# Projecting queries and keys by batch, 256 columns at a time, in the opening of two attentions

## The chip, the cores and the metric

The kernel runs on one core of a Trainium2 chip, all in float32 but for a few small bfloat16 terms. The metric is the device time of one execution in microseconds (us), taken as the median of several runs. Beside it stands one execution taken by the hardware profiler, from which every duration below comes. Engines are called as the profile calls them: PE (TensorE, matrix products), PEld (its weight loads, which overlap the products), DVE (VectorE), ACT (ScalarE), POOL (GpSimd) and SP (SyncE, which only issues transfers here).

## The reference

Two decoder layers on x of 8 batches x 256 tokens x 512 features, each step followed by a residual and a layer norm. What matters here is the first step of each layer:

```
def reference(x, ...):
    x = _layernorm(x + _L0_attn_ref(x, Wq, Wk, Wv, Wo, ...))     # first attention (differential)
    x = _layernorm(x + _L0_xattn_ref(...))                       # long convolution
    x = _layernorm(x + _L0_ffn_ref(x, ...))                      # mixture of experts, top 2 of 8
    x = _layernorm(x + _L1_attn_ref(x, w_qkv, w_o))              # self attention
    x = _layernorm(x + _L1_xattn_ref(...))
    x = _layernorm(x + _L1_ffn_ref(...))

# both attentions, per batch:
    q, k, v = projections of x          # 512 query features; keys and values 128 (first) or 512 (self)
    scores = q @ k.T * HD ** -0.5, masked above the diagonal
    out = softmax(scores) @ v           # first: attn1 - lambda * attn2, then an rms norm
    return out @ Wo.T
```

## The kernel before, in words

**Tiles.** The 2048 tokens are 16 tiles of 128 (`x[t]`), two tiles to a batch, and four tiles, which are two batches, to a group (`TPG` = 4, `GT` = 512 columns, `NG` = 4 groups, `S` = 256). To project a group, PE turns each of its tiles (`turned_group`, L194), ACT copies the turned tile into `xT` (L195; one buffer), and then a block of 128 features for the whole group is four products of 128x512 accumulated in PSUM (`feature_block`, L1404, through `product_steps`, L175) and evacuated by ACT (L1411). On PE each float32 product is two instructions in the profile. `token_block` makes the values of one tile.

**The attention loop.** `causal_attention` runs over units, a unit being some heads of one batch: 16 units to a group in the first attention (`upb` = 8 a batch), 8 in the self attention (`upb` = 4). A unit goes through `maxima` (L1151: scores `ps_q` on PE; L1160: ACT copies them into `rows`; L1162: POOL masks; L1171: DVE takes the maxima `neg`), some units later `weights` (L1214, L1223: scores again with the maxima subtracted, L1231: exponential on ACT, L1232 and L1242: mask and sum on POOL) and `products` (L1257, L1267: values and row sums on PE; L1275: DVE's reciprocal). The scores have one PSUM buffer. `rows` has two buffers in the first attention and one in the self attention, so there ACT's copy of a unit waits until DVE has reduced the unit before. After the maxima of a whole batch, DVE splits them (`split`) and PE turns them (`turn`, L1193).

**Order by hand.** Within the loop PE, DVE, ACT and POOL keep the order in which the program writes the instructions (`manual_schedule`); SP is free. Between the pieces of a unit, `fill(budget)` takes projection steps from `queue`, a list of pieces with the unit (slot) at which each is due; `MM` = 0.86 and `TR` = 0.45 are the costs that the planner counts for a product of 512 columns and a tile's transposes. `pressure` raises the budget when due times are near, `need(slot)` forces what is due, and `at(slots, place, f)` hangs a call on a later unit. `begin(g + 1)` puts the next group's pieces into the queue half way through a group. A queue that is empty leaves a unit with nothing between its parts.

**Opening of the first attention** (`diff_attention`). SP issues, in order: four x tiles (`load_x(range(TPG))`), Wk, Wq, Wv, Wo, small tables, the other twelve tiles. DVE and POOL reorder the columns of Wq once it is there (L269, L271). PE turns four tiles, projects the keys of the group (`ps_k`) and the first query block (`ps_f`), and begins the first unit's scores.

**Opening of the self attention.** Its x is not in SBUF: `combine` brings a tile back (`load`: x from `xd` through SP, L1075, and two gathers of 128 rows of the experts' results from `ys`, issued by POOL, L1077), adds the two results (`add`: DVE L1086, with the norm's moments and POOL's L139 and L140) and normalizes (`norm`: DVE L154). The first four tiles are brought before the loop begins, their steps interleaved; those of the next group hang on units of the loop:

```
        for steps in zip(*[arrive(t) for t in range(TPG)]):
            for f in steps:
                f()
...
                    first = max(0, 2 * KB * g - 1 + ti)
                    at(first - here, "end", load)
                    at(first - here + 1, "mid", lambda add=add: add(lambda f: at(0, "end", f)))
                    at(first - here + 2, "mid", norm)
```

Then come 4 query and 4 key blocks of 512 columns, due pairwise at units 0 to 3 of the group, and values due at 5 and 7 (9 in the last group).

Of the kernel before, what the change touches and what calls it, by code (L numbers as in the profile page):

```python
# [5 lines left out]


# [2 lines left out]

# [6 lines left out]
F32 = mybir.dt.float32  # L17
# [6 lines left out]
P = 128  # L24
B, S, D = 8, 256, 512
NT = B * S // P
TPG = 4
NG = NT // TPG
GT = TPG * P
KB = D // P  # L30
# [19 lines left out]
def decoder_kernel(ctx: ExitStack, tc: tile.TileContext, a: dict, out: bass.AP):  # L50
# [17 lines left out]
        for t in tiles:  # L68
            nc.sync.dma_start(out=x[t], in_=xin[:, t, :])

    load_x(range(TPG))

    ident = const.tile([P, P], F32, tag="ident", name="ident")
    make_identity(nc, ident)
# [97 lines left out]

    MM, TR = 0.86, 0.45

    def product_steps(tile, lhsT, rhs, done):  # L175

        ps = []

        def step(k):
            if k == 0:  # L180
                ps.append(tile())
            nc.tensor.matmul(  # L182
                ps[0], lhsT=lhsT(k), rhs=rhs(k), start=(k == 0), stop=(k == KB - 1)
            )
            if k == KB - 1:
                done(ps[0])

        return [(MM, lambda k=k: step(k)) for k in range(KB)]

    def turned(pools, dst, src, tag="mm"):  # L190

# [43 lines left out]
    def diff_attention():  # L235
# [6 lines left out]
        w = wpool.tile([P, 7168], F32, tag="w", name="w_l0")  # L242
        wk = load_w(w, 2048, a["L0_attn_Wk"], P)
        wq_in = load_w(w, 0, a["L0_attn_Wq"], D)
        wv = load_w(w, 2560, a["L0_attn_Wv"], P)
        wo = w[:, 3072:5120].rearrange("p (k c) -> p k c", k=KB)
        for t in range(4):
# [51 lines left out]
        def prepare(work, pools, g, at, here):  # L299
            qT = work.tile([P, KB, GT], F32, tag="qT", name="qT")  # L300
            kz = work.tile([P, 2, GT], F32, tag="kz", name="kz")
            v = work.tile([P, TPG, P], F32, tag="v", name="v", bufs=3)
            xT, need = turned_group(work, pools, g)

            def values(ti, ps=[]):
                if ti == 0:
# [7 lines left out]
                    nc.scalar.copy(v, ps.pop())  # L314

            values_steps = [(MM, lambda ti=ti: values(ti)) for ti in range(TPG)]
            if g:

                need.append((0, values_steps))

            def keys(ps):
                for i in range(2):
                    nc.scalar.mul(kz[:, i, :], ps, half[:, i : i + 1])

            need.append(
                (
                    0,
                    product_steps(
                        lambda: pools.tile([P, GT], F32, tag="mm", name="ps_k"),
                        lambda k: wk[:, k, :],  # L330
                        lambda k: xT[0][:, k, :],
                        keys,
                    ),
                )
            )
# [761 lines left out]
    def causal_attention(name, prepare, finish, upb=KB, gather=None):  # L1097
# [18 lines left out]
        with ExitStack() as st:  # L1116
# [176 lines left out]

            def at(slots, place, f):

                if place == "fill":
                    after.append((now[0] + slots, f))
                    after.sort(key=lambda piece: piece[0])
                else:
                    events.setdefault((now[0] + slots, place), []).append(f)  # L1300
# [100 lines left out]
                fill(9.0)  # L1401
                happen("end")

    def feature_block(pools, r, xT, w, at, c, scale=1.0):  # L1404

        cs = slice(at + c * P, at + (c + 1) * P)
        return product_steps(
            lambda: pools.tile([P, GT], F32, tag="mm", name="ps_f"),
            lambda k: w[:, k, cs],
            lambda k: xT[0][:, k, :],  # L1410
            lambda ps: nc.scalar.mul(r[:, c, :], ps, scale),  # L1411
        )

    def token_block(pools, xT, w, at, ti, done):
# [21 lines left out]

    def self_attention(wqkv, wo, arrive):

        for steps in zip(*[arrive(t) for t in range(TPG)]):
            for f in steps:  # L1440
                f()

        def prepare(work, pools, g, at, here):
            qT = work.tile([P, KB, GT], F32, tag="qT", name="qT")
            kT = work.tile([P, KB, GT], F32, tag="kT", name="kT")
            v = work.tile([P, TPG, D], F32, tag="v", name="v_s")
            xT, need = turned_group(work, pools, g)
            for c in range(KB):
                need.append((c, feature_block(pools, qT, xT, wqkv, 0, c, HD1**-0.5)))
                need.append((c, feature_block(pools, kT, xT, wqkv, D, c)))  # L1450

            if g + 1 < NG:
                for ti in range(TPG):
                    load, add, norm = arrive((g + 1) * TPG + ti)
                    first = max(0, 2 * KB * g - 1 + ti)
                    at(first - here, "end", load)
                    at(first - here + 1, "mid", lambda add=add: add(lambda f: at(0, "end", f)))
                    at(first - here + 2, "mid", norm)

            for ti in range(TPG):  # L1460
                need.append(
                    (
                        5 + ti // 2 * (4 if g == NG - 1 else 2),
                        token_block(
                            pools, xT, wqkv, 2 * D, ti,
                            lambda ps, ti=ti: nc.scalar.copy(v[:, ti, :], ps),
                        ),
                    )
                )
# [385 lines left out]
```

## Time and profile before

| | us |
|---|---|
| median of 3 runs | 2218.76 (2217.38 to 2219.33) |
| the profiled execution | 2202.62 |
| its span, first to last instruction | 2200.8 |
| PE busy in the span | 2053.4 (93%) |
| DVE, POOL, ACT busy | 1272.1, 824.4, 598.9 |
| first attention, about | 0 to 490 |
| self attention, about | 1114 to 1500 |
| one product pair of 128x512, out of `feature_block` | 0.86 |
| ACT: copy of scores (128x1536), exponential (128x1536), evacuation of 128x512, of 128x256 | 1.44, 1.45, 0.60, 0.37 |

The busy time of an engine counts its instructions from start to end; for PE the ends are modelled. A timeline row gives the start, the duration, the engine, the line, output and inputs, and in brackets how long the engine had been idle and what ended the wait. The granted clock of PE is given as a share of full speed, and its mean over the execution was 0.970.

### The profile page before, as it was taken

The page shows a single profiled execution, that of the slowest core. Times are in us where ns is not written, and L with a number is a line of the kernel's source. Part 1 is how long each engine was busy: PE and PEld are TensorE (multiplying, and loading weights), DVE is VectorE, ACT ScalarE, POOL GpSimd, SP SyncE. Part 2 cuts the span into 40 slices and gives each one's busy share as a digit, 9 for nine tenths or more (in the row PEclk, how much of TensorE's full clock was granted, in tenths as well). Part 3 has the DMA queues.
Part 4 walks back from the last instruction along what each step waited for, and adds up shares of the span by engine and source line. Part 5 has one row for each costly group of instructions (what it writes and reads, how often), then busy time and mean ns, then how long its engine had stood idle before and what let it go on. Part 6 is the DMA issues. An engine that isn't in the chain of part 4 may idle for free. (4 is left out here: it accounts for less than half of the span.)

```text
span 2200.8 us, 35612 instructions
## 1 busy us (share of the span) xinstructions
PE 2053.4 (93%) x14904; PEld 1192.7 (54%) x14904; DVE 1272.1 (58%) x1923; ACT 598.9 (27%) x723; POOL 824.4 (37%) x918
## 2 busy tenths in 40 slices
PE   7989899879999999999959999999999999999995
PEld 4545555544453455555524444446877875445543
DVE  4676767758888964222235746466344343476777
ACT  4545545520010013111114333340110110333342
POOL 2566767737556723000033644343000000242343
PEclk9989999989999999999989999999999999999998
DMA  6899801335124144131140201002100100000000
GB/s 221 328 385 382 312 1 45 92 87 198 29 76 164 29 148 149 62 141 61 48 145 29 77 20 58 1 2 96 39 20 20 39 0 1 1 11 11 11 18 33
DMA packets 110032, 197.56 MB, mean 90 GB/s; under 512 B 7088, under 2 KB 30768, under 8 KB 109872
## 3 DMA queue, kind: packets, MB, share of 16 engines
q1 hardware_dynamic: 104752, 178.49, 23.4%
q0 software_dynamic: 5120, 16.78, 2.2%
q8 instruction: 120, 1.97, 0.4%
q14 instruction: 40, 0.33, 0.0%
HBM read 93.54 MB, written 112.20 MB: 93 GB/s over the span
## 5 line engine op out<-in xcount | busy, mean ns | idle before, releaser
L1275 DVE RECIPROCAL rsum<-ps_pv 128x256 f32<-128x256 f32 x128 | 224.4, 1753 | 238.1 <-PE ps_pv L1267 237.9
L171 PE MATMUL ps_y<-kv,wt 128*128 128x512 f32 x640 | 282.6, 600 | 4.4 <-POOL kv L519 3.8
L1231 ACT ACTIVATE pT<-ps_k 128x1536 f32<-128x1536 f32 x128 | 185.7, 1450 | 288.9 <-PE ps_k L1223 286.9
L1171 DVE TENSOR_REDUCE neg<-rows 128x12 f32<-128x1536 f32 x128 | 223.1, 1743 | 50.9 <-POOL rows L1162 50.9
L1160 ACT COPY rows<-ps_q 128x1536 f32<-128x1536 f32 x128 | 184.2, 1439 | 184.0 <-PE ps_q L1151 142.2
L1162 POOL TENSOR_SCALAR_AFFINE_SELECT rows<-rows 128x1024 f32<-128x1024 f32 x128 | 140.1, 1094 | 250.3 <-ACT rows L1160 250.0
L1232 POOL TENSOR_SCALAR_AFFINE_SELECT pT<-pT 128x1024 f32<-128x1024 f32 x128 | 141.1, 1102 | 242.9 <-ACT pT L1231 242.9
L171 PEld LDWEIGHTS ps_y<-kv,wt 128*128 128x128 f32 x640 | 120.9, 192 | 154.4 <-issue 135.8
L1242 POOL TENSOR_TENSOR pT<-pT 128x512 f32<-128x512 f32 x112 | 145.2, 1296 | 9.3
L1077 POOL DMA_INDIRECT w_l1x<-ys,slots x32 | 32.9, 1028 | 267.1 <-DMA ys<-y_m 259.2
L182 PE MATMUL ps_t<-w_l1f,xT 128*128 128x512 f32 x256 | 122.0, 611 | 0.0
L182 PE MATMUL ps_f<-xT,w_l1a 128*128 128x512 f32 x256 | 118.2, 604 | 2.9 <-ACT xT L195 2.9
L992 PE MATMUL po_m<-dn,hT 128*128 (+1 forms) x216 | 101.9, 609 | 1.5
L139 POOL TENSOR_SCALAR rstd<-bn_mv 128x1 f32<-128x1 f32 x80 | 16.9, 212 | 217.0 <-DVE bn_mv L145 211.2
L1267 PE MATMUL ps_pv<-pT,ones_v 128*32 128x256 f32 (+1 forms) x1152 | 85.0, 377 | 6.7 <-POOL pT L1242 6.3
L557 DVE TENSOR_REDUCE yc<-z 128x64 f32<-128x512 f32 x128 | 86.0, 673 | 6.2 <-POOL w_l1a L558 5.8
L1151 PE MATMUL ps_q<-kz,qT 32*128 32x128 f32 x1536 | 62.9, 294 | 22.6 <-ACT pT L1231 17.5
L1151 PEld LDWEIGHTS ps_q<-kT,qT 32*128 32x128 f32 x1536 | 49.9, 190 | 56.2 <-issue 17.0
L1151 PEld LDWEIGHTS ps_q<-kz,qT 32*128 32x128 f32 x1536 | 50.4, 192 | 54.8 <-ACT pT L1231 34.4
L182 PEld LDWEIGHTS ps_f<-xT,w_l1a 128*128 128x128 f32 x256 | 46.3, 189 | 54.8 <-issue 49.3
L1151 PE MATMUL ps_q<-kT,qT 32*128 32x128 f32 x1536 | 62.4, 292 | 12.5 <-ACT kT L1411 4.8
L974 DVE TENSOR_TENSOR h_b<-h_b,pg 128x352 f32<-128x352 f32 x36 | 18.8, 521 | 95.3 <-ACT h_b L973 95.3
(326 smaller groups left out, 3744.6 us busy)
## 6 DMA issues: line engine op xcount, KB each, us to landing
xs<-zero SPq DMA_DIRECT2D x8, 4352.0 KB, 31.3
ys<-zero SPq DMA_DIRECT2D x8, 4352.0 KB, 31.4
filters<-in_L_xattn_k SPq DMA_DIRECT2D x4, 2560.0 KB
first_h<-xs SPq DMA_DIRECT2D x36, 256.0 KB, 2.6
ys<-y_m SPq DMA_DIRECT2D x36, 256.0 KB, 2.0
gu<-in_L_ffn_gate_up_proj SPq DMA_DIRECT2D x3, 2816.0 KB, 19.8
wt<-filters SPq DMA_DIRECT2D x32, 256.0 KB, 2.8
x<-in_x SPq DMA_DIRECT2D x16, 256.0 KB, 4.9
```

Of the source, the lines that this page charges most:

```text
L171: nc.tensor.matmul(ps, lhsT=lhsT(k), rhs=rhs(k), start=(k == 0), stop=(k == n - 1))
L182: nc.tensor.matmul(ps[0], lhsT=lhsT(k), rhs=rhs(k), start=(k == 0), stop=(k == KB - 1))
L557: nc.vector.tensor_reduce(yc[:, lb], z, AX.X, ALU.add)
L992: nc.tensor.matmul(po, lhsT=hT[:m, i, :], rhs=dn[i][:m, bass.ds(e, 1), :], start=(i == 0), stop=(i == len(FCH) - 1),)
L1151: nc.tensor.matmul(block[:, s, j, :], lhsT=q(rows, c, b * S + i * P, P), rhs=k(rows, c, b * S + keys * P, P), start=True, stop=True,)
L1160: nc.scalar.copy(d.rearrange("p j s k -> p s j k"), block)
L1162: nc.gpsimd.affine_select(out=rows, in_=rows, compare_op=ALU.is_ge, fill=-FAR, base=0, pattern=[[0, 8], [-1, P]], channel_multiplier=1,)
L1171: return lambda: nc.vector.tensor_reduce(neg[u // upb % 2][:, :, :, c], d, AX.X, ALU.max, negate=True)
L1231: nc.scalar.activation(p[:, 0:3].rearrange("p j s q -> p s j q"), block, AF.Exp)
L1232: nc.gpsimd.affine_select(out=p[:, 0:2].rearrange("p j s q -> p (j s) q"), in_=p[:, 0:2].rearrange("p j s q -> p (j s) q"), compare_op=ALU ...
L1242: nc.gpsimd.tensor_tensor(p[:, 3], p[:, 1], p[:, 2], ALU.add)
L1275: nc.vector.reciprocal(r, ps[:, 1, :])
```

## The change

Queries (in all groups of both attentions) and keys (in the first attention's first group, in all groups of the self attention) are projected for one batch at a time: the same products with 256 columns instead of 512, twice as many, each half evacuated by itself. The second batch's halves are due later, eight units in the first attention and four in the self attention. In the first attention only two tiles are loaded ahead of Wk and Wq, tiles 2 and 3 behind them. In the self attention only tiles 0 and 1 are brought before the loop, in an order written out for DVE and POOL; tiles 2 and 3 are brought by units 0 to 2, and those of group 1 one tile a unit, at units 1 to 4 instead of 0, 0, 1, 2. Pieces whose tiles are not there yet are put into the queue at a later unit (`hold`, by way of a new place, "due mid", which sorts them in by due time).

```diff
@@ decoder_kernel
-    load_x(range(TPG))
+    load_x(range(2))
@@ product_steps
-    def product_steps(tile, lhsT, rhs, done):
+    def product_steps(tile, lhsT, rhs, done, cost=MM):
...
-        return [(MM, lambda k=k: step(k)) for k in range(KB)]
+        return [(cost, lambda k=k: step(k)) for k in range(KB)]
@@ diff_attention
         wq_in = load_w(w, 0, a["L0_attn_Wq"], D)
+        load_x(range(2, TPG))
         wv = load_w(w, 2560, a["L0_attn_Wv"], P)
...
+            def keys(tokens):
+                def done(ps):
+                    for i in range(2):
+                        nc.scalar.mul(kz[:, i, tokens], ps, half[:, i : i + 1])
+
+                n = tokens.stop - tokens.start
+                return product_steps(
+                    lambda: pools.tile([P, n], F32, tag="mm", name="ps_k"),
+                    lambda k: wk[:, k, :],
+                    lambda k: xT[0][:, k, tokens],
+                    done,
+                    MM * n / GT,
+                )
+
             if g:
...
-            for c, first in enumerate((0, 1, 4, 5)):
-                need.append((first, feature_block(pools, qT, xT, wq, 0, c, HD0**-0.5)))
-
-            if g == 0:
-                need.append((9, values_steps))
+                need = turns + [(0, values_steps), (0, keys(slice(0, GT)))]
+            else:
+                need = turns[:2] + [(0, keys(batches[0]))]
+                need += [(3, steps) for _, steps in turns[2:]]
+                need += [(8, keys(batches[1])), (9, values_steps)]
+            for b, tokens in enumerate(batches):
+                for c, first in enumerate((0, 1, 4, 5)):
+                    block = feature_block(pools, qT, xT, wq, 0, c, HD0**-0.5, tokens)
+                    need.append((8 * b + first, block))
+            need.sort(key=lambda piece: piece[0])
@@ causal_attention
-                if place == "fill":
+                if place == "due mid":
+                    at(slots, "mid", lambda: insort(queue, f, key=lambda piece: piece[0]))
+                elif place == "fill":
@@ feature_block
-    def feature_block(pools, r, xT, w, at, c, scale=1.0):
+    def feature_block(pools, r, xT, w, at, c, scale=1.0, tokens=slice(0, GT)):
...
+        n = tokens.stop - tokens.start
         return product_steps(
-            lambda: pools.tile([P, GT], F32, tag="mm", name="ps_f"),
+            lambda: pools.tile([P, n], F32, tag="mm", name="ps_f"),
             lambda k: w[:, k, cs],
-            lambda k: xT[0][:, k, :],
-            lambda ps: nc.scalar.mul(r[:, c, :], ps, scale),
+            lambda k: xT[0][:, k, tokens],
+            lambda ps: nc.scalar.mul(r[:, c, tokens], ps, scale),
+            MM * n / GT,
         )
@@ self_attention
-        for steps in zip(*[arrive(t) for t in range(TPG)]):
-            for f in steps:
-                f()
+        with tc.manual_schedule(engines={mybir.EngineType.DVE, mybir.EngineType.Pool}):
+            first = [arrive(t) for t in range(2)]
+            for load, _, _ in first:
+                load()
+            roots = []
+            for _, add, _ in first:
+                add(roots.append)
+            for root, (_, _, norm) in zip(roots, first):
+                root()
+                norm()
...
+            def arriving(t, slot, place):
+                load, add, norm = arrive(t)
+                at(slot - here, place, load)
+                at(slot - here + 1, "mid", lambda: add(lambda f: at(0, "end", f)))
+                at(slot - here + 2, "mid", norm)
...
+            hold = {(0, 1): 2, (1, 0): 5, (1, 1): 6}
+            need = []
+            for b in range(2):
+                tokens = slice(b * S, (b + 1) * S)
+                pieces = [(b * KB, steps) for _, steps in turns[2 * b : 2 * b + 2]]
+                for c in range(KB):
+                    slot = b * KB + c
+                    pieces.append(
+                        (slot, feature_block(pools, qT, xT, wqkv, 0, c, HD1**-0.5, tokens))
+                    )
+                    pieces.append((slot, feature_block(pools, kT, xT, wqkv, D, c, 1.0, tokens)))
+                late = 9 if g == NG - 1 else 7
+                for ti in range(2 * b, 2 * b + 2):
+                    pieces.append(value(ti, late if b else 5))
+                pieces.sort(key=lambda piece: piece[0])
+                if g == 0 and b == 1:
+                    for t in range(2, TPG):
+                        arriving(t, 0, ("start", "end")[t % 2])
+                if (g, b) in hold:
+
+                    for slot, steps in pieces:
+                        at(hold[g, b] - here, "due mid", (2 * KB * g + slot, steps))
+                else:
+                    need += pieces
+            need.sort(key=lambda piece: piece[0])
 
             if g + 1 < NG:
                 for ti in range(TPG):
-                    load, add, norm = arrive((g + 1) * TPG + ti)
...
+                    arriving((g + 1) * TPG + ti, 1 + ti if g == 0 else 2 * KB * g - 1 + ti, "end")
```

More of the change, by code (lines that the diff above doesn't have):

```diff
@@ L8 @@
 import math
+from bisect import insort
 from contextlib import ExitStack
@@ L302, in prepare @@
             v = work.tile([P, TPG, P], F32, tag="v", name="v", bufs=3)
-            xT, need = turned_group(work, pools, g)
+            xT, turns = turned_group(work, pools, g)
+            batches = [slice(b * S, (b + 1) * S) for b in range(2)]
             def values(ti, ps=[]):
@@ L316, in prepare @@
             values_steps = [(MM, lambda ti=ti: values(ti)) for ti in range(TPG)]
-            if g:
[L319 to L330, printed above, removed]
-                        lambda k: xT[0][:, k, :],
[L332 to L335, printed above, removed]
-            for c, first in enumerate((0, 1, 4, 5)):
-                need.append((first, feature_block(pools, qT, xT, wq, 0, c, HD0**-0.5)))
-            if g == 0:
-                need.append((9, values_steps))
+            def keys(tokens):
[10 more added lines that the diff above has]
+                )
+            if g:
+                need = turns + [(0, values_steps), (0, keys(slice(0, GT)))]
[8 more added lines that the diff above has]
+            need.sort(key=lambda piece: piece[0])
             if g == NG - 1:
@@ L1402, in causal_attention @@
                 happen("end")
-    def feature_block(pools, r, xT, w, at, c, scale=1.0):
+    def feature_block(pools, r, xT, w, at, c, scale=1.0, tokens=slice(0, GT)):
         cs = slice(at + c * P, at + (c + 1) * P)
+        n = tokens.stop - tokens.start
         return product_steps(
-            lambda: pools.tile([P, GT], F32, tag="mm", name="ps_f"),
+            lambda: pools.tile([P, n], F32, tag="mm", name="ps_f"),
             lambda k: w[:, k, cs],
-            lambda k: xT[0][:, k, :],
-            lambda ps: nc.scalar.mul(r[:, c, :], ps, scale),
+            lambda k: xT[0][:, k, tokens],
+            lambda ps: nc.scalar.mul(r[:, c, tokens], ps, scale),
+            MM * n / GT,
         )
@@ L1446, in prepare @@
             v = work.tile([P, TPG, D], F32, tag="v", name="v_s")
[L1447 to L1450, printed above, removed]
+            xT, turns = turned_group(work, pools, g)
+            def arriving(t, slot, place):
[3 more added lines that the diff above has]
+                at(slot - here + 2, "mid", norm)
@@ new lines, in value @@
+            def value(ti, slot):
+                return slot, token_block(
+                    pools, xT, wqkv, 2 * D, ti, lambda ps: nc.scalar.copy(v[:, ti, :], ps)
+                )
[8 more added lines that the diff above has]
+                        (slot, feature_block(pools, qT, xT, wqkv, 0, c, HD1**-0.5, tokens))
+                    )
+                    pieces.append((slot, feature_block(pools, kT, xT, wqkv, D, c, 1.0, tokens)))
[11 more added lines that the diff above has]
+                    need += pieces
@@ L1452, in prepare @@
+            need.sort(key=lambda piece: piece[0])
             if g + 1 < NG:
                 for ti in range(TPG):
-                    load, add, norm = arrive((g + 1) * TPG + ti)
[L1455 to L1469, printed above, removed]
+                    arriving((g + 1) * TPG + ti, 1 + ti if g == 0 else 2 * KB * g - 1 + ti, "end")
```

## The prediction

> **What bounds it now.** I read the busy shares first, then the stretches, then TensorE's own timeline for gaps. TensorE (PE) is busy 93% of the 2200.8 us span; the next engine, DVE, 58%. The chain of waits reaches back only to 1505 us, so it covers neither stage that the change touches; there the idle time of PE has to be read row by row. The stretches show where it lies (columns: stretch, its length, busy us of PE, PEld, DVE, ACT, POOL with instructions, granted clock, DMA share, GB/s):
>
> ```profile
> 0.00:20.00 20.00, 14.10 (x36) 7.32 (x40) 3.70 (x18) 5.49 (x8) 4.16 (x24) 1.00 0.74 185
> 40.00:60.00 20.00, 14.51 (x176) 12.07 (x175) 12.17 (x12) 11.62 (x12) 5.71 (x6) 0.74 0.52 207
> 1100.00:1150.00 50.00, 27.76 (x104) 14.24 (x103) 14.39 (x31) 7.62 (x14) 13.02 (x17) 0.80 0.41 148
> 1600.00:1700.00 100.00, 99.81 (x428) 78.12 (x429) 41.40 (x72) 9.90 (x21) 6.96 (x15) 1.00 0.07 21
> ```
>
> The openings of the two stages have holes; a stage in flow has none. The timeline of PE names them (start, us, instruction, in brackets idle before and what ended it):
>
> ```profile
> 9.12 6.56 PE L182 MATMUL ps_k<-xT,w_l 128*128 128x512 f32 x8 [0.67 <-ACT xT L195]
> 19.80 0.95 PE L1151 MATMUL ps_q<-kz,qT 32*128 32x128 f32 x24 [0.69 <-ACT qT L1411]
> 46.44 1.67 PE L1151 MATMUL ps_q<-kz,qT 32*128 32x128 f32 x24 [1.56 <-ACT rows L1160]
> 51.63 0.40 PE L1193 MATMUL ps_n<-ident_b,terms 128*32 128x128 bf16 x8 [1.62 <-DVE terms L1182]
> 245.57 0.95 PE L1151 MATMUL ps_q<-kz,qT 32*128 32x128 f32 x24 [1.61 <-ACT pT L1231]
> 1135.01 3.48 PE L194 MATMUL pt<-ident,x 128*128 128x128 f32 x16 [20.61 <-DVE x L154]
> 1146.98 0.95 PE L1151 MATMUL ps_q<-kT,qT 32*128 32x128 f32 x24 [0.69 <-ACT kT L1411]
> 1198.57 3.70 PE L182 MATMUL ps_f<-xT,w_l1a 128*128 128x512 f32 x8 [1.44 <-ACT xT L195]
> 1253.55 1.35 PE L1151 MATMUL ps_q<-kT,qT 32*128 32x128 f32 x24 [1.55 <-ACT pT L1231]
> ```
>
> The first unit of scores (ps_q) waits till 19.80, and the self attention stands 20.6 us for four normed tiles. Rows like 245.57 and 1253.55 are units that have no projection work left to lay beside ACT's exponentials. PE work is otherwise fixed, so **the change is worth the PE idle time that it removes, less what it adds**.
>
> **A. Opening of the first attention.** Before, four tiles are loaded ahead of Wk and Wq. Issue plus time to landing: Wk 2.67 + 5.3 = 7.97, Wq 3.15 + 8.8 = 11.95. So 1 MB of Wq took 4.0 us, and the two tiles (0.5 MB) now put behind it are worth 2.0; Wq lands between 9.05 (issue 0.9 earlier as well) and 9.95; I take 9.8. POOL's four reordering copies for the first columns (288 ns each) end at 11.0. PE meanwhile: the transposes of tiles 0 and 1 end at 5.65, their copies at 6.28; half of ps_k (half of 6.56) fills 6.5 to 9.8, and PE waits for 11.0. Then half of the first query block. Its price depends on the clock. In the trace ps_k's weight loads take 337 ns against 190 later, from 9.12 to 15.1, though the clock column shows 1.00 there: half speed for 6.4 us of unbroken work. The Trainium skill ("TensorE: Matmul & The Clock Gate", Part 1: The HAM clock gate) says about 3.4 us of sustained work release it. By the page the block ends at 12.8, by the row (half speed until 6.5 + 6.4 = 12.9) at 13.7. I go by the row: evacuation 0.4, first scores at 14.2 against 19.80.
>
> From there the order of the changed program gives the projection work between one unit's scores and the next: 2.3, 2.8, 2.2, 2.6, 1.8, 1.9, 2.6, 1.3 us (256-column product 0.43 us, value projections 0.6 us a tile), plus 0.88 for each ps_q: the eighth scores start at 36.5, the ninth at 39.1 against 46.44. Before, the same work ran out after the sixth unit, and PE then moved at ACT's 2.5 us a unit; that hole also took the clock to 0.50 from 46 to 55 us, about 1.8 us on the path. The next wait stays: ps_n needs the eighth unit's maxima, 36.5 + 1.0 (end of ps_q) + 1.44 (copy) + 1.1 (mask) + 1.75 (reduce) + 1.6 (split) = 43.4, against 51.63. PE idles 2.3 there instead of 1.62. **A: -8.5** (-5 to -10).
>
> **B. The rest of the first attention.** Query halves for the second batch are due eight units later, so the planner spreads them. In its order, the units of the second and third group that had 1.46, 0.6 and 1.46 us of such work now have 2.3 or more; the idle rows there (239.77 to 257.92, 349.04 to 357.83) sum to 4.1 + 3.0. The empty units of the first group (0, 0.6, 0.6 us) stay. Against it: 1.7 us more is left after the last scores, and the split itself. Its pitch is read from the cross attention's same shape, 24.17 us for 112 of 128x256 = 0.215 each, against 0.427 for 128x512 (7.00 us for 16, less the last one's tail): 0.003 a pair, 136 pairs, 0.4 us. Evacuations cost ACT 0.37 twice instead of 0.60, under PE's work (ACT is busy half the time). 7.1 - 1.7 - 0.4 = 5.0, of which I take two thirds, since new short waits are likely. **B: -3.2** (0 to -5).
>
> **C. Opening of the self attention.** Gathers for tiles 0 and 1 start at 1118.02 as before, 1.26 apart on POOL. By DVE's rows they land at 1122.9, 1126.1, 1127.5, 1128.3; the sixteen x loads keep the DMA full in both versions. Now DVE norms two tiles without the others between: moments of tile 1 end at 1130.2, its norm at 1131.9; PE's first transpose 1130.85 instead of 1135.01; first product 1133.85 instead of 1139.16. It starts partly at half clock (the transposes before ran at 0.50): +1.0.
>
> Then a new limit. A unit has only 3.45 us of products instead of 6.9, and DVE's queue, kept in program order, puts tiles 2 to 5 between the units' reductions. There is one buffer of rows, so ACT's copy of unit u waits for DVE's reduction of u-1, and everything behind it in ACT's queue waits too, the copies of xT included. Worked through with gathers landing 3.5 us after issue (1150.78 to 1154.26 in the trace, DMA otherwise idle):
> unit 0: scores 1138.8, reduce ends 1144.2;
> unit 1: scores 1143.5; adds and moments of tiles 2 and 3 till 1149.1; reduce ends 1150.9;
> unit 2: scores 1148.3, ACT's copy held to 1150.9; tile 4 till 1154.5; reduce ends 1156.3;
> unit 3: scores 1153.3, copy held to 1156.3 and done 1157.8; the xT copies behind it end 1159.0.
> PE has turned tiles 2 and 3 by 1155.4 and stands 3.65 us. Fifth scores start at 1165.9 with six half blocks (10.3 us) still owed, that is 1176.2 against 1177.59: of five microseconds gained, 1.4 are left. **C: -1.4** (+5 to -6: below, if the gathers land after 6.7 us as the first ones did; above, if DVE's order costs less than I fear).
>
> The page's rule that one idle window of about 3.4 us brings back half clock speaks against this change here: it would cost 1.7 us more. The trace already shows a fall to 0.58 (1254 to 1258) after gaps of 0.69, 0.34 and 1.55, but also 1.00 after the same gaps at 1345. I leave it to the range.
>
> **D. The rest of the self attention.** Before, PE's idle rows from 1198 to 1500 sum to 12.4 us, among them three units with no projection at all (2.6 each, around 1250, 1343, 1432). The new order has no unit below 3.8 us. But tiles are now turned two at a time with the product right behind: three times after scores or an exponential on ACT (pt 1.2 us beside 1.45 + 1.16 of ACT: 1.65 idle), three times otherwise 0.65, and some 2.0 of the old short waits: 8.9. The clock dips at 1254 and 1434 took 1.7 each; I count 1.0 back. The split is 256 pairs, 0.8. 12.4 - 8.9 + 1.0 - 0.8 = 3.7; I take 3. **D: -3** (0 to -6).
>
> **Sum:** -8.5 - 3.2 - 1.4 - 3.0 = -16.1. The profiled execution took 2202.62, so it would take 2186.5; the runs shown have their median 16 us higher, 2218.76, and I put the same difference there: **2202.7 us**. Other stages keep their instructions and move earlier as a block; the DMA is saturated from 100 to 200 us by zero fills that nobody awaits.
>
> **Rivals.**
> 1. Forecast, 2197 to 2208: 0.58.
> 2. The self attention's new queue bites harder: gathers of tiles 3, 4, 5 land after 6.7 us instead of 3.5 and the clock falls. C becomes +5: 2209. For it: 6.7 us was seen under load. Against it: the x loads are over by 1136. 0.16.
> 3. The first attention does not pass its gain on, because ACT and POOL pace its units (POOL's 3.5 us, ACT's 2.9 and DVE's 4 against 6.7 for a unit speak against): only C and D remain, 2214. 0.13, half of it no change.
> 4. No stall in the self opening, C -6 and D -6: 2195. 0.07.
> 5. **Slower:** 256-column products paced by their weight loads. A load takes 190 ns and the product 215, only 25 ns of cover; if ACT's or DVE's traffic stretched the pitch beyond 0.2355, the 784 halves would eat the 16.1, and at 0.245 add 23.5: 2226. Against it stands 1600 to 1700, PE 99.8% busy at exactly this shape. 0.06.
>
> What a measurement can tell from no change is about 0.2%, 4.4 us. Faster by more: 0.58 + 0.16 + 0.06 + 0.07 = 0.87; within 0.07; slower 0.06. The range, 2192 to 2214, leaves out rival 5 and the ends of 3 and 4.
>
> **What would show it.** First scores near 14 and ninth near 39 (A); clock 1.00 from 40 to 60; no waits of ps_q for pT near 238 to 250 (B); first product of the self attention about 20 us after the last po_m instead of 25, and an idle row of 3 to 4 us before its second batch's first ps_f, ended by ACT's xT (C); no ps_q pair with nothing between (D). Wrong if the 256-column pitch is above 0.22 us, or the first scores are not 4 us earlier.

## The result

Over 20 runs each the kernel before took 2215.72 us and the changed one 2207.3 (2198.62 to 2218.05). The ratio is 0.996, its 95% interval 0.9948 to 0.9972: 8.4 us less (6.2 to 11.5), a little more than half of the 16.1 forecast.

The windows of the changed kernel (columns as in the prediction's table of stretches):

```profile
0.00:20.00 20.00, 14.30 (x89) 10.71 (x90) 4.36 (x18) 6.58 (x10) 5.40 (x25) 1.00 0.67 185
40.00:60.00 20.00, 16.68 (x218) 13.21 (x220) 9.02 (x11) 10.99 (x13) 7.42 (x7) 0.91 0.52 206
1100.00:1150.00 50.00, 30.79 (x141) 19.66 (x140) 13.71 (x27) 8.51 (x15) 11.45 (x13) 0.76 0.42 147
1600.00:1700.00 100.00, 99.81 (x423) 77.10 (x422) 41.87 (x74) 10.71 (x22) 7.69 (x17) 1.00 0.07 21
```

The hole from 40 to 60 us has shrunk (PE 16.68 busy instead of 14.51, the clock 0.91 instead of 0.74). From 1100 to 1150 PE has 3.0 us more busy time, but at 0.76 of the clock instead of 0.80. The control, 1600 to 1700, is the same. The timeline of PE at the same places:

```profile
15.14 0.95 PE L1158 MATMUL ps_q<-kz,qT 32*128 32x128 f32 x24 [0.47 <-ACT qT L1422]
26.39 0.95 PE L1158 MATMUL ps_q<-kz,qT 32*128 32x128 f32 x24 [0.97 <-ACT rows L1167]
43.26 0.95 PE L1158 MATMUL ps_q<-kz,qT 32*128 32x128 f32 x24
48.18 0.30 PE L1200 MATMUL ps_n<-ident_b,terms 128*32 128x128 bf16 x8 [2.94 <-DVE terms L1189]
...
243.34 0.95 PE L1158 MATMUL ps_q<-kz,qT 32*128 32x128 f32 x24
...
849.09 5.36 PE L999 MATMUL po_m<-dn,hT 128*128 x6 [10.47 <-ACT hT L992]
...
1131.98 2.29 PE L195 MATMUL pt<-ident,x 128*128 128x128 f32 x8 [17.24 <-DVE x L155]
1134.95 6.65 PE L183 MATMUL ps_f<-xT,w_l1a 128*128 128x256 f32 x16 [0.67 <-ACT xT L196]
1142.08 0.95 PE L1158 MATMUL ps_q<-kT,qT 32*128 32x128 f32 x24 [0.47 <-ACT kT L1422]
1142.96 3.72 PE L183 MATMUL ps_f<-xT,w_l1a 128*128 128x256 f32 x16
1164.00 5.79 PE L183 MATMUL ps_f<-xT,w_l1a 128*128 128x256 f32 x16 [4.73 <-ACT xT L196]
1204.76 1.56 PE L183 MATMUL ps_f<-xT,w_l1a 128*128 128x256 f32 x6 [1.51 <-ACT xT L196]
```

The first scores come 4.7 us earlier, the ninth 3.2, ps_n 3.5. The wait of ps_q for pT near 245 is gone. In the self attention the first transpose waits 17.24 us instead of 20.61, so it comes 3.4 us earlier behind the last po_m. But the first block of products runs cold, at half the clock for most of its length (6.65 us; the same 16 take 3.72 in the row at 1142.96), and before the second batch's products PE stands 4.73 us and then runs cold again (5.79).

**One row has to be set aside.** At 849.09, in the expert stage, which the change doesn't touch, PE stood 10.47 us, and so the traced span of the changed kernel (2203.7) is longer than that of the one before (2200.8). The kernels below were measured in four later groups, each beside runs of the kernel before. In the groups where before's median was 2202.4 and 2203.0 no trace has this row, before's own included. Where it was 2216.3 and 2212.1 every trace has it, at some 10.5 and some 6.8 us. So, by the medians, it goes with the occasion and not with the change, though no trace of the kernel before comes from an occasion that shows the row; before's first trace, 2202.62 us against 2211.21 as the lowest of the 20 runs above, is one without it. I therefore compare stages, not spans. Four marks serve, all read from PE's timeline: the start of the first scores; the start of the first ps_n; the end of the first attention (the start of the pt that waits about 4.16 us for first_h); the self attention, from the end of the last po_m to the first ps with w_l1x.

| us, mean (range) | as before | as changed | difference | predicted |
|---|---|---|---|---|
| first scores | 19.2 (18.4 to 19.8), 3 traces | 14.0 (13.2 to 15.1), 7 traces | -5.2 | -5.6 |
| first ps_n (A) | 50.95 (49.9 to 51.6) | 47.1 (46.2 to 48.2) | -3.8 | -8.2 |
| end of the first attention (A and B) | 486.4 (484.9 to 487.8) | 475.2 (470.2 to 478.6) | -11.2 | -11.7 |
| self attention (C and D) | 392.7 (391.3 to 393.5), 3 traces | 393.1 (392.7 to 393.7), 6 traces | +0.4 | -4.4 |

The traces are those of the two kernels and of the experiments that leave the stage in question as it is in one of them.

### The profile page after: what moved, and what is told of

Its sections match the earlier page's. It is cut to its first block, busy times and chain, and to the rows that moved or that the text cites. A ratio compares the mean times of both kernels' runs of the same rounds, so it can differ in the third digit from the quotient of the medians.

```text
span 2203.7 us, 36445 instructions
## 1 busy us (share of the span) xinstructions
PE 2054.0 (93%) x15296; PEld 1264.8 (57%) x15296; DVE 1275.9 (58%) x1923; ACT 605.1 (27%) x773; POOL 826.9 (38%) x918
## 5 line engine op out<-in xcount | busy, mean ns | idle before, releaser
L183 PE MATMUL ps_f<-xT,w_l1a 128*128 128x256 f32 x512 | 129.2, 400 | 12.2 <-ACT xT L196 12.2
L183 PEld LDWEIGHTS ps_f<-xT,w_l1a 128*128 128x128 f32 x512 | 96.9, 197 | 33.8 <-ACT xT L196 14.3
L999 PE MATMUL po_m<-dn,hT 128*128 (+1 forms) x216 | 104.4, 621 | 12.0 <-ACT hT L992 10.5
L183 PE MATMUL ps_f<-xT,w_l 128*128 128x256 f32 x256 | 71.2, 406 | 0.9 <-POOL w_l L273 0.7
```

The lines of the kernel that those rows point to most:

```text
L183: nc.tensor.matmul(ps[0], lhsT=lhsT(k), rhs=rhs(k), start=(k == 0), stop=(k == KB - 1))
L999: nc.tensor.matmul(po, lhsT=hT[:m, i, :], rhs=dn[i][:m, bass.ds(e, 1), :], start=(i == 0), stop=(i == len(FCH) - 1),)
```

## The experiments

**Which stage pays.** Two kernels each take one half of the change. The first keeps the first attention as changed:

```diff
@@ self_attention (all of it as before the change)
+        for steps in zip(*[arrive(t) for t in range(TPG)]):
+            for f in steps:
+                f()
...
+            xT, need = turned_group(work, pools, g)
```

> The first attention and its loads as in the changed kernel; the self attention as before it (512 columns, four tiles normed first). My theory after the two traces: all of the gain is made in the first attention and is passed on, and the self attention gives 2 to 3 us of it back. Then this kernel takes 10 to 11 us off (ratio 0.9951 to 0.9955), more than the full change does (0.996), the last transposes of the first attention end near 477 us instead of 488, and the self attention takes 391 us from the last po_m to the first ps with w_l1x, as before. Rival, as the prediction had it: both stages gain, the self attention some 4 us, and then this kernel takes off only some 4 of the 8.4 us (ratio 0.998). Rival 3 of the prediction (the first attention's gain is not passed on): ratio 0.9995 to 1.0005. In the traced execution of the full change TensorE stood 10.47 us in the expert stage, before a po_m that waited for ACT's hT; nothing of the change lies there. If that is a chance of one execution, no such row is in this trace; if the earlier start of the stages causes it, it is here again.

Measured: 2195.48 us against 2202.38, ratio 0.9964 (0.995 to 0.9977). The first attention ends at 478.59, and the row in the expert stage is not there. The whole gain is in this half. The size I expected from the first pair of traces, 10.6 us (0.9952), lies at the interval's edge; 7.9 was measured by the ratio. Its self attention, before's own code, took 393.42 us where the first trace had 391.27: the 2.5 us that the first two traces set between the versions were mostly scatter.

The second is the other half, with all four tiles of x loaded ahead again and the first attention's projections at 512 columns:

```diff
-    load_x(range(2))
+    load_x(range(TPG))
@@ diff_attention (prepare as before the change; self_attention as changed)
```

> The first attention as before, with its four tiles loaded ahead; the self attention as in the changed kernel (256 columns, two tiles first, the others between the units). My theory: slower by 2 to 3 us (ratio 1.0008 to 1.0014), with the same rows as in the full change: a cold first block of about 6.6 us, a wait of ACT's copies of rows for DVE's reduction, an idle row of 4 to 5 us before the second batch's first ps_f, and about 393.5 us from the last po_m to the first ps with w_l1x. Rival, as the prediction had it: faster by some 4 us (ratio 0.998); then the 2.5 us of the traced execution belong to that execution, not to the change.

Measured: ratio 1.001 (0.9994 to 1.0027), self attention 392.66 us, with the cold first block and a stall of 3.81. A gain of 4 us is excluded; a small loss and nothing can't be told apart.

**The halves without the two-tile opening.**

```diff
-        with tc.manual_schedule(engines={mybir.EngineType.DVE, mybir.EngineType.Pool}):
...
+        for steps in zip(*[arrive(t) for t in range(TPG)]):
+            for f in steps:
+                f()
...
-            hold = {(0, 1): 2, (1, 0): 5, (1, 1): 6}
+            hold = {}
...
-                    arriving((g + 1) * TPG + ti, 1 + ti if g == 0 else 2 * KB * g - 1 + ti, "end")
+                    arriving((g + 1) * TPG + ti, max(0, 2 * KB * g - 1 + ti), "end")
```

The tiles of group 1 come at units 0, 0, 1 and 2 again, too.

> As the changed kernel, but the self attention brings and norms all four tiles of the first group before its first product, as before the change; its projections stay in halves of 256 columns, and no tile of group 0 has to come between its units. This parts the two halves of the self attention's edit. If the two-tile opening is what costs (my theory: cold first block +2.9, the 4.73 us stall and the cold stretch after it +2.1, against 4.2 us of earlier start), this kernel loses the 4 us of early start but has no stall: the first product comes 25 us after the last po_m, no idle row before the second batch's first ps_f is over 1 us, and the self attention takes 389 to 392 us; ratio 0.994 to 0.9955. If the halves themselves cost (more switches, more evacuations, the same work in another order), the self attention takes 393 us or more and the ratio is 0.996 or above.

Measured: self attention 390.65 us, inside the range of the first theory, but ratio 0.9982 (0.997 to 0.9995), outside it; in this trace the stages behind the self attention took 694.5 us where most take 685.5 (see the last section), and the traced time, 2197.39, is close to the median. And PE did stand before the second batch, 2.63 us, though all its tiles were normed long before: ACT's copies of xT waited behind a copy of rows, and that for DVE. So the halves bring a part of the stall by themselves.

**DVE's order.**

```diff
-                at(slot - here + 1, "mid", lambda: add(lambda f: at(0, "end", f)))
-                at(slot - here + 2, "mid", norm)
+                at(slot - here + later, "mid", lambda: add(lambda f: at(0, "end", f)))
+                at(slot - here + later + 1, "mid", norm)
...
-            hold = {(0, 1): 2, (1, 0): 5, (1, 1): 6}
+            hold = {(0, 1): 1, (1, 0): 5, (1, 1): 7}
```

(later is 0 for tiles 2 and 3, which are loaded at the start of unit 0; 2 for the tiles of group 1; 1 elsewhere.)

> As the changed kernel, but in the self attention tiles 2 and 3 are gathered right behind tiles 0 and 1 and added one unit earlier on DVE, ahead of the first two reductions, their transposes are due one unit earlier, and the adds of tiles 4 to 7 come one unit later. My theory: the stall of 4.73 us before the second batch's first ps_f comes from DVE's queue (reductions behind the adds, ACT's copies of rows behind the reductions, the copies of xT behind those); with the adds ahead of the reductions the stall falls below 2 us, the stretch behind it does not run at half clock, and the self attention takes 388 to 391 us; ratio 0.9935 to 0.995. Rival: the gathers and the cold clock set the time, not DVE's order; then first scores come later by as much as the stall gets shorter, the self attention stays at 393 us and the ratio at 0.996. A second rival: the adds, now ahead of the first reduction, hold the first units back, and the stall only moves to the second or third unit's rows.

Measured: ratio 0.9979 (0.9969 to 0.999), self attention 393.08 us. The stall before the second batch fell to 0.72, and one of 4.48 opened 43 us later, before group 1. The timelines of ACT and of PE in this kernel, there:

```profile
1189.46 1.44 ACT L1167 COPY rows<-ps_q 128x1536 f32<-128x1536 f32 x1 [3.29 <-DVE neg L1178]
1190.80 1.08 ACT L196 COPY xT<-pt 128x512 f32<-128x512 f32 x2
...
1191.93 1.22 PE L183 MATMUL ps_f<-xT,w_l1a 128*128 128x256 f32 x2 [4.48 <-ACT xT L196]
```

It is the same chain in another place, as the second rival said, though further on than it put it: DVE's reduction behind later tiles' adds, ACT's rows behind the reduction, xT behind the rows, PE behind xT. In the changed kernel ACT's timeline reads:

```profile
1154.69 1.44 ACT L1167 COPY rows<-ps_q 128x1536 f32<-128x1536 f32 x1 [2.52 <-DVE neg L1178]
1161.54 1.44 ACT L1167 COPY rows<-ps_q 128x1536 f32<-128x1536 f32 x1 [4.29 <-DVE neg L1178]
1162.87 1.08 ACT L196 COPY xT<-pt 128x512 f32<-128x512 f32 x2
```

**Cutting the chain at two of its links.** The changed kernel ran again beside the next three:

> The changed kernel once more, unchanged, so that the next three stand beside it on the same chip. Ratio 0.996 as before (0.995 to 0.997). The row of 10.47 us in the expert stage, which none of the four experiments so far has shown, is not in this trace; then the trace is some 8 to 11 us shorter than the one before, by a ratio of the spans of about 0.996.

Measured: ratio 0.9962 (0.9945 to 0.9978), self attention 392.81 us with a stall of 4.72. The expectation on the expert stage was wrong: the row is there, 10.54 us.

A second buffer of rows:

```diff
-                d = work.tile([P, 3, 4, P], F32, tag="rows", name="rows", bufs=1 if name == "s" else 2)
+                d = work.tile([P, 3, 4, P], F32, tag="rows", name="rows", bufs=2)
...
-                done = lambda ps, t=t0 + i: add_norm_later(work, t, ps, at)
+                done = lambda ps, t=t0 + i: add_norm_later(work, t, ps, at, 2)
```

(The last line leaves `res` two buffers instead of three.)

> As the changed kernel, with a second buffer for rows in the self attention (one of the three buffers of res is given up for it). ACT's copy of a unit's scores then no longer waits for DVE's reduction of the unit before. My theory: the 3.8 to 4.7 us that TensorE stands before the second batch's first ps_f come from that wait (ACT rows held 2.52 and 4.29 us, the copies of xT queued behind). Then this row falls below 1.5 us, ACT's rows waits of that length are gone from the stretch, and the self attention takes 389 to 391 us instead of 392.7 to 393.7. Rival: DVE is late in itself with the adds and norms of tiles 2 and 3, so the transposes wait for their tiles and the stall stays at 3 us or more under another name (pt for DVE x); the self attention then stays at 392 to 394 us. Either way the time of the whole moves by 0.1% at most.

The transposes of a group's second two tiles due earlier:

```diff
-                pieces = [(b * KB, steps) for _, steps in turns[2 * b : 2 * b + 2]]
+                pieces = [(b * 2.5, steps) for _, steps in turns[2 * b : 2 * b + 2]]
```

> As the changed kernel, but in the self attention the transposes of each group's second two tiles are due a unit and a half earlier, so that the first batch's last products lie between them and the first product that needs their copies. My theory of the small gain after the opening: the idle did not fall (13.6 to 12 or 13 us) because each pair of tiles is now turned with the product right behind, and TensorE stands for ACT's copies of xT: 1.5 and 0.73 us in the first groups, 0.85 and 0.72 us in the others. Of these the four before a second batch (4.7 in the opening, 0.73, 0.85, 0.72) go or shrink, the 1.5 before a first batch stay, and the idle after the opening falls from about 12 to 9.5 or 10. The self attention takes 390 us or less. Rival: the copies stay behind rows and exponentials on ACT wherever they are put; then the idle stays within 0.7 us of the changed kernel's.

PE's timeline with two buffers of rows, then with the earlier transposes:

```profile
1157.33 1.10 PE L195 MATMUL pt<-ident,x 128*128 128x128 f32 x8
1160.90 3.72 PE L183 MATMUL ps_f<-xT,w_l1a 128*128 128x256 f32 x16 [2.47 <-ACT xT L196]
```

```profile
1150.44 0.66 PE L195 MATMUL pt<-ident,x 128*128 128x128 f32 x4 [0.53 <-DVE x L155]
1151.44 0.65 PE L195 MATMUL pt<-ident,x 128*128 128x128 f32 x4 [0.34 <-DVE x L155]
1151.93 1.89 PE L183 MATMUL ps_f<-xT,w_l1a 128*128 128x256 f32 x8
1154.30 0.95 PE L1158 MATMUL ps_q<-kT,qT 32*128 32x128 f32 x24 [0.47 <-ACT kT L1422]
1155.18 3.72 PE L183 MATMUL ps_f<-xT,w_l1a 128*128 128x256 f32 x16
```

With two buffers ACT's waits for DVE are gone and the stall halves, to 2.47, not below the 1.5 I expected: the rest is that the tiles are turned right ahead of their products, with a 1.44 us copy of rows ahead of xT's copies. With the earlier transposes two waits of 0.53 and 0.34 are left, although ACT's rows still wait 2.52 and 2.10 for DVE: products that need no new xT now lie between. In both no 16 products of this stretch take over 3.72 us, where the changed kernel's took 5.79. The self attention takes 386.63 and 386.49 us, 6 us less than in the changed kernel beside them. Of this 1.6 and 1.2 us lie ahead of the first scores, where neither edit alters anything (the first block ran cold for less long there, 5.42 and 5.28 us in all against 6.31); from the first scores on it is 361.4 and 360.9 us against 366.0, so that the edits are worth 4.6 and 5.1. The ratio of the whole is 0.995 (0.9932 to 0.9968) and 0.9955 (0.9938 to 0.9971), which doesn't part them from 0.9962. From the fifth scores on the idle rows stayed (11.4 and 12.3 us against 11.8 in the trace beside them): there the rival of the earlier transposes was right, as rows of 0.73 and 0.86 ended by xT became 1.40 and 1.22 ended by kT.

**The opening of the first attention.** The lambda exponential later, Wq's copies alternating:

```diff
-        nc.scalar.activation(lam[:, 0:2], lam[:, 0:2], AF.Exp)
...
+                at(4, "mid", lam_sums)
+                at(6, "mid", lam_exp)
...
-                if i % 2:
+                if (i + k) % 2:
                     nc.vector.tensor_copy(dst[:, k], src[:, k])
```

> As the changed kernel, but the exponential of the lambdas is issued in the sixth unit instead of ahead of all, and the reordering copies of Wq alternate between DVE and POOL within each column block instead of by block. Theory: in the opening of the first attention the idle row of 0.97 to 1.22 us before the third or fourth scores (ACT's copy of rows stood behind the exponential, which waited for DVE) is gone, and the wait of the first query block for POOL falls from 0.7 to 0.2 or less; first scores near 13.5, and ps_n comes 1 to 1.5 us earlier (45.5 to 46.5). The rest of the three microseconds that the opening lost against my prediction (value projections of 0.98 us a tile, a ps_n that waits 2.9 for DVE's terms) stays. Rival: ACT's in-order queue is not what delays the scores, since DVE's reductions pace them; then the row only moves to the next unit and ps_n stays at 46.2 to 48.2.

Measured: the row of 0.97 is gone, and from the first to the eighth scores it takes 24.57 us instead of 25.61. The alternating copies gave nothing (the wait for POOL is 0.64 against 0.71), so ps_n stands at 47.15: 32.0 us behind the first scores instead of 33.0. Ratio 0.9965 (0.9944 to 0.9987), no difference from the changed kernel.

The loads in their old order, the halves kept:

```diff
-    load_x(range(2))
+    load_x(range(TPG))
...
-        load_x(range(2, TPG))
```

> As the changed kernel, but all four tiles of the first group are loaded ahead of Wk and Wq, as before the change; the halves stay. This parts step A into the order of the loads and the halves. My theory: Wq lands near 12 us instead of 10.4, and its first block of columns is ready 1.5 us later; the clock's cold stretch is over at the same time, so the first scores come 1 to 1.5 us later than in the changed kernel (13.2 to 15.1), near 15.3, against 19.8 of the kernel before: the halves are worth some 4 of the 5.5 us, the order of the loads 1.5. Ratio 0.9965 to 0.997. Rival: the order of the loads is what makes the early start; then the first scores come at 17.5 or later.

Measured: first scores at 16.37, between theory and rival. By this one trace the order of the loads is worth 2.4 of the 5.2 us and the halves 2.8; the seven traces with the changed opening spread over 2 us. At the end of the first attention (477.2) and in the time (0.9964, 0.9943 to 0.9984) no loss can be seen; where those 2.4 us went is open.

**The later groups of the first attention** at 512 columns again:

```diff
-            for b, tokens in enumerate(batches):
+            for b, tokens in enumerate([slice(0, GT)] if g else batches):
```

> As the changed kernel, but in the first attention only the first group's queries come in halves; the later groups project 512 columns at once, due as before the change. My theory: step B (the later groups) is a gain of its own, about 5 us of TensorE idle between 200 and 460 us: the rows of ps_q that waits for ACT's pT near 236, 242, 254 and 345, 351 come back, the idle from 200 to 460 us rises from 15 to 17 to some 20 to 21, and the first attention ends 4 to 6 us later than the changed kernel's (472 to 478), near 480; ratio 0.9975 to 0.9985. Rival: the opening alone makes the gain; then this kernel ends the first attention where the changed one does, ratio 0.996.

PE's timeline of this kernel:

```profile
234.32 0.95 PE L1158 MATMUL ps_q<-kz,qT 32*128 32x128 f32 x24 [0.64 <-ACT pT L1238]
240.13 0.95 PE L1158 MATMUL ps_q<-kz,qT 32*128 32x128 f32 x24 [1.61 <-ACT pT L1238]
253.67 0.95 PE L1158 MATMUL ps_q<-kz,qT 32*128 32x128 f32 x24 [1.02 <-ACT pT L1238]
```

The waits are back. PE's idle in the last 290 us of the first attention is 30.3 us, as in the three traces with before's first attention (30.1 to 31.3), against 24.5 to 26.7 in the seven with the changed one. The stage ends at 481.49, later than in any of the seven; ratio 0.9988 (0.9968 to 1.0008). B is a gain of its own.

**The expert stage, and a faster version.** The kernel before, traced once more, and the changed kernel with the three edits above together (two buffers of rows, earlier transposes, the later exponential with the alternating copies):

> The kernel before the change, unchanged, once more traced. Every trace of the changed kernel and of its variants on the first and the third chip has a row of 10.5 us in the expert stage (po_m after hT), and no trace of the second chip has it, whatever the kernel. My theory: it belongs to the chip or the session, not to the change. Then this trace has the row if the kernel beside it on the same chip has it, and lacks it if that one lacks it; the stretch from the first attention's end to the last po_m takes some 637 or some 626 us in both. Rival: it comes from the earlier start of the changed kernel's stages on some chips; then this trace lacks it where the one beside it has it.

> The changed kernel with the three edits together: a second buffer of rows in the self attention, the second two tiles of a group turned a unit and a half earlier, the lambda exponential issued in the sixth unit and the copies of Wq alternating. Theory: with a stall in the opening gone and ACT no longer held by rows, the self attention takes 384.5 to 386.5 us (386.6 and 386.5 for either edit alone, so they share most of their gain, the stall of 4.7), the first attention is as in the changed kernel less 0.5 to 1 us; ratio 0.992 to 0.9945, against 0.996 for the changed kernel. Rival: the edits help only in a trace, as chance of the clock; ratio 0.9955 to 0.9965.

Neither trace has the row in the expert stage; that it would stand in before's trace on another occasion is inferred from the medians, not traced. The chip does not decide it, which the expectation left possible: this group and the one with 2212.1 ran on the same chip, one without the row and one with it. The combined kernel took 2187.95 us against 2203.01, ratio 0.9932 (0.9911 to 0.9952). It beats the kernel before by 15.1 us; from the changed kernel (0.9948 to 0.9972) its interval is not quite parted, but the traces agree: the self attention takes 385.9 us, 358.1 of them from the first scores on (366.0 and 366.4 in the two traces of the changed kernel), and ps_n comes at 45.44. In this kernel the stall is a wait of 0.75.

## Why the prediction was right and wrong

**A: right in kind, half the size.** First scores were put at 14.2 and came at 14.0. From there the eighth scores were to take 22.3 us and took 25.6, and ps_n another 7.4 instead of 6.9. The largest term is the price of a value projection, put at 0.6 us a tile. The timelines, of the kernel before and of the changed one:

```profile
36.94 2.05 PE L171 MATMUL ps_v<-w_l,xT 128*128 128x128 f32 x16
```

```profile
30.94 2.94 PE L172 MATMUL ps_v<-w_l,xT 128*128 128x128 f32 x24
```

Eight records are a tile, so a tile costs 0.98: four tiles, 1.5 us. It stood in before's trace. The second term is a wait that I did not look for. ACT's timeline of the changed kernel:

```profile
24.81 0.20 ACT L295 ACTIVATE lam<-lam 128x2 f32<-128x2 f32 x1 [2.63 <-DVE lam L294]
24.92 1.42 ACT L1167 COPY rows<-ps_q 128x1536 f32<-128x1536 f32 x1
```

With the scores earlier, the exponential of lambda stands in ACT's queue among them and waits for DVE, with a unit's rows behind it: 0.97 us of PE, which moving it took away. The other 0.8 us up to the eighth scores I did not split. Three figures of the working were slips that do not matter here: half speed from 9.12 to 15.1 is 6.0 us and not 6.4, its own steps put the ninth scores at 38.7 and not at 39.1, and ps_n at 43.4 makes A -8.2 and not -8.5.

**B: the step that was cut failed, not the one that was worked.** From ps_n to the end of the stage the changed kernel gains 7.4 us in the mean. The working gave 5.0, and I took two thirds because new short waits seemed likely. They did not come: the idle time of this stretch (its length less PE's busy time) fell by 4.7. The rest is mostly the clock. Here is this stretch in the kernel before and in the one with the first attention alone:

```profile
51.63:483.63 432.00, 391.01 (x5168) 227.55 (x5168) 294.89 (x321) 215.77 (x203) 284.64 (x267) 0.96 0.57 205
```

```profile
47.78:474.42 426.64, 392.82 (x5264) 243.73 (x5264) 295.29 (x321) 217.03 (x215) 286.26 (x267) 0.96 0.58 210
```

At 0.96, the clock of the three traces with before's first attention, stand three of the seven changed ones (those of this kernel, of DVE's order and of the two buffers); they gain 4.5 us here and end the stage at 478.2 in the mean, 8.2 us earlier. The other four ran at 0.97 and 0.98. A and B together were forecast at -11.7 and are -11.2, but that is luck: A fell short, B at an equal clock is -4.5, and some 3 us came with a higher clock, which the working did not have. Whether the change raises it is open.

**C: the step that failed.** At the fifth scores the self attention stands 57.8 us behind the last po_m instead of 64.7 (means of six and three traces); with my six half blocks of 10.3 us still owed, C is +3.4 instead of -1.4. The mechanism was as described: one buffer of rows, ACT held, xT behind it. The stall was put at 3.65 and is 3.8 to 4.7. What I mis-sized is the clock. The cold start was put at +1.0 and makes 2.9 at the first block (6.65 against 3.72), and behind the stall another 2.1 (5.79 against 3.72), which the sum left out. That is 4.0 of the 6.9 us by which the changed kernel's fifth scores came later than worked out (58.4 behind the last po_m instead of 51.5); 1.1 is the longer stall, and 1.8 I did not split. I had weighed the page "TensorE: Matmul & The Clock Gate" of the Trainium skill (Part 1: an idle window of about 3.4 us brings half clock back) at 1.7 us and left it to the range. At this place the page was right: behind gaps of 3.81 and more the products ran cold, behind 2.47 and 2.63 they did not. It is not the whole rule: in the kernel before the clock was 0.58 from 1254 to 1258 behind gaps of 1.55 us at most.

**D: the size was right, its terms were not.** The stage from the fifth scores on, in the kernel before and in the changed one:

```profile
1177.59:1505.67 328.08, 312.92 (x2809) 155.04 (x2809) 194.31 (x249) 120.18 (x123) 140.71 (x154) 0.99 0.10 30
```

```profile
1173.15:1508.49 335.34, 321.58 (x3049) 198.81 (x3049) 197.37 (x247) 125.41 (x153) 144.33 (x159) 1.00 0.10 31
```

That is 7.3 us more; less the 10.3 owed it is -3.0, as forecast, and the three and the six traces agree within 0.1 us. But the terms are not those of the working. The idle time of PE (the length less PE's busy time) fell by 1.4 us, where 3.5 was worked out. PE's busy time, less the 10.3, fell by 1.6, where the working had 0.2 (1.0 back from the clock, 0.8 lost to the split): both dips of the clock, near 1254 and 1434, are gone, in all six traces, and not a part of them.

**The rivals.** Rival 2 had the size (C at +5, total 2209) and half of the mechanism: the clock fell, but no gather was late; DVE waited 0.27 us at most for one between 1146 and 1162. Rival 3 falls with the half that keeps the first attention. Rival 4 did not come, nor would it have with the two edits that cut the chain: with both the self attention gains 6.8 us, not 12. Rival 5 falls with the pitch: in the changed kernel 16 instructions of 128x256 take 3.72 us and 8 take 1.99, so each further one takes 0.216, under the 0.22 that was the limit.

**The sum.** By stages -10.8, by time -8.4 (6.2 to 11.5). With the first attention at before's clock the stages give -7.8. Both lie in the interval, so no further step has to be found.

## What to carry to other kernels

Halving a product lets work start on half of its data and gives a planner smaller pieces for its holes, but it also halves the cover that each unit has: work out the chain of in-order queues behind that cover, and cut it by putting products that need nothing new between a transpose and its first reader, rather than by reordering the late work on another engine, which here only moved the stall. Before pricing a stall, ask whether it is long enough to take the clock: here 4.73 us of waiting cost 6.8.

## What was not expected of the hardware

The clock falls in some executions and not in others, at the same gaps. The stretches from 115 to 125, 125 to 135 and 155 to 165 us in the two traces of the changed kernel, the first and then the second (PEclk is the last column but two):

```profile
115.00:125.00 10.00, 8.36 (x104) 5.37 (x100) 5.37 (x5) 2.89 (x2) 8.07 (x7) 0.67 1.03 383
125.00:135.00 10.00, 6.76 (x117) 4.55 (x109) 6.67 (x7) 4.85 (x4) 6.12 (x6) 0.72 1.04 382
155.00:165.00 10.00, 8.37 (x130) 5.75 (x132) 6.71 (x9) 6.87 (x8) 6.45 (x8) 1.00 1.03 380
```

```profile
115.00:125.00 10.00, 6.73 (x116) 4.50 (x111) 7.13 (x7) 4.84 (x4) 7.66 (x8) 0.83 1.04 384
125.00:135.00 10.00, 8.02 (x137) 4.49 (x132) 5.92 (x6) 4.48 (x4) 9.37 (x9) 1.00 1.04 382
155.00:165.00 10.00, 8.38 (x103) 6.18 (x101) 5.88 (x8) 6.22 (x8) 4.89 (x7) 0.83 1.03 381
```

None of the gaps in these stretches is longer than 1.64 us, and the four longest, of 1.61 to 1.64 us between 111 and 135 us, stand at matching places of both traces. The page named under C calls the clock's window free-running, so that its place against the work differs from run to run; that fits, but no run here shows that it is the cause. The scatter goes through every stage: the unaltered stages behind the self attention, to PE's last instruction, took 685.3 to 685.8 us in eight of the fourteen traces, 689.0 to 694.5 in four, and 682.3 and 687.1 in the others; the four all have the first attention changed, and their mean clock from 1800 to 2100 us is 0.94 to 0.95, against 0.97 in both of the kernel before. Whether the earlier start invites that or chance does is open. The time of a run goes with its mean clock: a straight line through the 67 runs of the kernel before beside the first four kernels gives 1.6 us for 0.001 (an estimate). The cause of the row of 6.8 to 10.5 us in the expert stage is open too.
